# An RWKV and Hadamard feed-forward block: the third token form's down product is split once more, and the next tokens' chores move between engines

## The chip, the cores and the metric

The kernel runs on one core of a Trainium2 chip. A core has TensorE (matmuls into eight PSUM banks of 128 partitions x 512 fp32), VectorE, ScalarE, GpSimd, and SyncE, which here does nothing but issue DMAs. Each works through its own queue in order and waits on semaphores for the others. The metric is the device time of one execution in microseconds (us), as the median of several runs. The times spoken of inside an execution come from one profiled run.

In the profile the engines are PE (TensorE matmul), PEld (TensorE weight load), DVE (VectorE), ACT (ScalarE), POOL (GpSimd) and SP (SyncE). All instructions are recorded under line 34, since a small wrapper issues them, so the tile names tell them apart.

## The reference

Input x is 4 batches x 2048 tokens x 512 channels, fp32. Output is x plus an attention branch plus a feed-forward branch, both of the layer norm of x:

```python
xn = layernorm(x)                                   # over the 512 channels
shifted = xn, one token later (zero before the first)
xr, xk, xv = (mu * xn + (1 - mu) * shifted for mu in (mu_r, mu_k, mu_v))
r, k, v = xr @ Wr.T, xk @ Wk.T, xv @ Wv.T           # 512 x 512 each
wkv = recurrence over time of (k, v) with decay w and bonus u
attn = (sigmoid(r) * wkv) @ Wo.T
hidden = silu(xn @ W1.T) * (xn @ W3.T)              # 2048 wide
ffn = fwht(hidden) @ W2.T                           # Walsh-Hadamard, then back to 512
out = x + attn + ffn
```

## The kernel before

The 8192 tokens go through in eight blocks of 1024 (`TB`), with channels on partitions (`xnT`) and tokens along the free dimension. Matmuls are fp32; each matmul of the source is two in the trace. The Hadamard transform is folded into the second feed-forward weight in block 0, which also stores derived weights in HBM (`part_w`, `down_w`); block 1 derives and stores `deep_w`. From block 2 on all weights are only loaded.

Products of a 2 x 2 split (channels by tokens) are done with seven instead of eight block products, in the manner of Strassen and Winograd (`seven`, line 333): sums of the token quarters on the right, sums of weight quarters on the left, and the partial results passed between PSUM banks by ScalarE copies.

A block has two stages.

**Up stage.** In blocks 1 to 7 first six projected pairs (`projected_pair`, line 391; two each of k, v and r), then sixteen gate and linear tiles (`up`, line 421). Each of these 22 takes 28 matmuls of 512 columns. Between them, in small pieces handed out by `step` and `hook`, VectorE and ScalarE mix the tokens for v and r (`mix_before` on ScalarE, then `mix_here` on VectorE, then four differences in `mix_forms`) and run the recurrence (`wkv`, line 247, nine pieces for each of four channel groups). GpSimd makes the four token forms of the gate and linear tiles in `tf` (`token_forms`, line 310). Every tile loads the weights of the second next into a ring of three (`ring_a`). The results stand in `right`: sixteen units of gated hidden values and four of attention values (`r_of`), that is two halves of ten units, each by two token halves, named y11, y12, y21, y22.

**Down stage.** These 20 units are contracted to the 512 outputs, again with a seven-product split. In block 0 (`down_whole`, line 617) each of the seven is done whole, as four pieces of weights with five matmuls of 512 columns each. In blocks 1 to 7 (`down`, line 706) five of the seven (d0 to d4, class `Deep`, line 667) are split once more into seven products of 256 columns, each one piece of weights; the other two, T1 (form 0) and T3 (form 3), are done whole. `DEEP` (line 511) lists the weight forms that are split. The order of pieces is written out by hand in `program` (line 535), and the order of everything else in the body of `down`: `forms` are VectorE differences of 128 x 1280 elements, `step` is one product with its ScalarE copy, `clear` zeroes half a bank by ScalarE, `onto` adds a finished result (one PSUM addition of 512 columns and one of 256 from `s5`) to the output slots x11, x12, x22, x21, and `store` writes a slot out. Weights of the down stage come through a ring of eight pieces, `pieces_w`: at product u, piece u + 7 is asked for, once product u - 1 has left its slot.

The next block's tokens are prepared during the down stage by a generator, `next_tokens`, advanced at set places by `advance`. VectorE takes the statistics from `x_tok`, which lies in `k_sb` (`token_statistics`, line 144: bn_stats, bn_aggr, one power by GpSimd), two DMAs pass them through HBM and spread them over all partitions into `v_sb` (`statistics`, line 159), VectorE normalises `xnT` (eight pieces), mixes k's tokens into `tf` and makes three of their four forms.

All DMAs are issued by SyncE in the order of the program, so a DMA that has to wait holds those after it.

Of the kernel before, what the change touches and what calls it, by code (L numbers as in the profile page):

```python
# [1 line left out]

# [6 lines left out]
F32 = mybir.dt.float32  # L9
# [30 lines left out]
def tile_rwkv_attn_hadamard_ffn(  # L40
# [38 lines left out]
    deep_w = dram.tile([5, 7, P, QR, P], F32, name="deep_w")  # L79
# [39 lines left out]
    x_tok = k_sb.rearrange("p b t -> p (b t)").rearrange("p (t c) -> p t c", c=C)  # L119
# [4 lines left out]
    mix_of = {1: tf.rearrange("p f k t -> p (f k t)").rearrange("p (b t) -> p b t", t=TB)}  # L124
    mix_of[2], mix_of[0] = right[:, 0, 0:NB, :], right[:, 0, NB : 2 * NB, :]
    t4_of = {kind: unit(NP + n) for n, kind in enumerate((1, 2, 0))}
# [32 lines left out]
    def statistics(i):  # L159
        rs = token_statistics(i, x_tok)  # L160
        sp.dma_start(out=stat_d[i].rearrange("s (p t) -> p s t", p=P), in_=rs)
        sp.dma_start(out=spread, in_=stat_d[i].unsqueeze(0).to_broadcast([P, 2, TB]))

# [17 lines left out]
    def load_first_tokens(t, m):  # L181
        src = x[ds(t * P, m * P), :].rearrange("(t p) c -> p t c", p=P)
        sp.dma_start(out=x_tok[:, t : t + m, :], in_=src)

    def first_statistics(half):
        return token_statistics(f"f{half}", x_tok[:, half * HT : (half + 1) * HT, :])
# [123 lines left out]
    def token_forms():  # L310
        sub = ALU.subtract
        pool.tensor_tensor(t1, b12, b11, sub)
        pool.tensor_tensor(t2, b22, t1, sub)
        pool.tensor_tensor(t3, b22, b12, sub)
        pool.tensor_tensor(t4, b21, t2, sub)
# [195 lines left out]
    DEEP = (1, 4, 6, 5, 2)  # L511
# [24 lines left out]
    for m, n in ((1, 1), (2, 0), (1, 2), (2, 1), (1, 3), (1, 4), (2, 2), (1, 5), (2, 3), (2, 4), (2, 5), (1, 6), (2, 6)):  # L536
        program += deep(m, n)
    for m, n in ((3, 0), (3, 1), (4, 0), (3, 2), (4, 1), (3, 3), (3, 4), (4, 2), (3, 5), (4, 3), (4, 4), (3, 6), (4, 5)):
        program += deep(m, n)
    p7 = plain(3)  # L540
    program += [p7[0], *deep(4, 6), *p7[1:]]
# [75 lines left out]
    def down_whole(i, advance, next_parts):  # L617
# [8 lines left out]
        advance(1)  # L626
        next_parts()

# [7 lines left out]
        advance(8)  # L636
# [4 lines left out]
        advance(4)  # L641
# [9 lines left out]
        advance(3)  # L651
# [6 lines left out]
        advance(7)  # L658
# [8 lines left out]
    class Deep:  # L667
        def __init__(self, down, m, banks_of, rights, slots):
            self.m = m
            self.down, (self.a, self.b, self.f), self.q, self.t = down, banks_of, rights, slots  # L670
            self.s5 = small.tile([P, H // 2], F32, tag="s5", name=f"s5_{down.i}_d{m}")

        def clear(self):
            for pt in (self.a, self.f):
                act.activation(pt[:, lo], had_sb.unsqueeze(1).to_broadcast([P, 2, P]), AF.Copy, scale=0.0)
# [25 lines left out]
        def onto(self, slots, *which):  # L701
            for g in which:
                add(slots[g], (self.a, self.b)[g])
                dve.tensor_tensor(slots[g][:, hi], slots[g][:, hi], self.s5, ALU.add)

    def down(i, advance, next_parts, last):
# [4 lines left out]
        free = [s.rearrange("p f k c -> p (f k c)")[:, 0 : QR * (H // 2)].rearrange("p (q t) -> p q t", q=QR) for s in (  # L711
            ring_a.tile([P, 7, KH, P], F32, tag="a", name=f"right_{i}_{n}") for n in range(3))]
        k_flat, tf_flat = k_sb.rearrange("p b t -> p (b t)"), tf.rearrange("p f k t -> p (f k t)")
        in_k, in_tf = (
            [flat[:, ds(n * QR * H // 2, QR * H // 2)].rearrange("p (q t) -> p q t", q=QR) for n in range(3)]
            for flat in (k_flat, tf_flat)
        )
        d0 = Deep(d, 0, sets[0], y21, [*free, in_tf[0]])
        d1 = Deep(d, 1, sets[1], y11, [*in_k, in_tf[1]])
        d2 = Deep(d, 2, sets[0], y22, [*free, in_tf[2]])  # L720
        d3 = Deep(d, 3, sets[1], y22, [*in_k, y22[2]])
        d4 = Deep(d, 4, sets[0], y21, [*free, y21[2]])

        def forms(out, x0, x1, n):
            difference(out[n], x0[n], x1[n])

        def first(g, rh):
            d.plain_step(0, g, rh, pa, (0, 0), True)

# [7 lines left out]
        d1.clear()  # L737
        add(x11[0], pa[0])
        advance(1)
        d0.step(0, 1)  # L740
        first(1, 0)
        for n in (0, 1):
            forms(y11, y12, y11, n)
        d1.forms(0)
        d0.step(2)
        for n in (0, 1):
            forms(y12, y22, y12, n)
        first(1, 1)
        add(x11[1], pa[1])
        for g in range(KH):  # L750
            act.copy(u2_of[g], pa[g])
        for n in (2, 3):
            forms(y11, y12, y11, n)
        d1.forms(1)
        d0.step(3, 4)
        d0.onto(x11, 0)
        d1.forms(2, 3)
        d0.step(5)
        d1.step(0)
        d0.step(6)  # L760
        for n in (2, 3):
            forms(y12, y22, y12, n)
        d2.forms(0)
        d0.onto(x11, 1)
        d2.clear()
        d2.forms(1)
        d1.step(1)
        d2.step(0)
        d2.forms(2, 3)
        d1.step(2)  # L770
        d2.step(1)
        d1.step(3, 4)
        for n in (0, 1):
            forms(y22, y22, y11, n)
        for g in range(KH):
            d.store(x11[g], 0, g, 0)
        d1.onto(x12, 0)
        d1.onto(x22, 0)
        d2.step(2)
        d3.forms(0)  # L780
        d1.step(5)
        advance(2)
        d2.step(3)
        forms(y22, y22, y11, 3)
        d2.step(4)
        forms(y22, y22, y11, 2)
        d2.onto(x12, 0)
        d.residual(x21, 1, 0)
        d2.step(5)
        d3.clear()  # L790
        for n in (0, 1):
            forms(y21, y21, y22, n)
        d1.step(6)
        d1.onto(x12, 1)
        d1.onto(x22, 1)
        d2.step(6)
        d2.onto(x12, 1)
        d3.step(0)
        d4.clear()
        d3.step(1)  # L800
        d3.forms(1)
        d4.forms(0)
        d4.step(0)
        for n in (3, 2):
            forms(y21, y21, y22, n)
# [5 lines left out]
        advance(2)  # L811
        d3.step(4)
        d3.forms(3)
        d4.step(2)
        d4.forms(2)
        d3.onto(u2_of, 0)
        act.copy(pa[0], u2_of[0])
        d3.step(5)

        def c12(g):  # L820
            add(x12[g], u2_of[g])
            d.store(x12[g], 0, g, 1)

        c12(0)
        d4.step(3)
        advance(2)
        d4.step(4)
        d4.forms(3)
        d3.step(6)
        d3.onto(u2_of, 1)  # L830
        act.copy(pa[1], u2_of[1])
        c12(1)
        d4.step(5)
        d4.onto(x21, 0)
        d.plain_step(3, 0, 0, pa, (0, 1))
        advance(2)
        d4.step(6)
        d4.onto(x21, 1)
        next_parts()
        advance(7)  # L840

        def ends(pt, g, cols=whole):
            for slots, half in ((x22, 1), (x21, 0)):
                add(slots[g], pt, cols)
                d.store(slots[g], 1, g, half, cols)

        d.plain_step(3, 0, 1, pa, (0, 1))
        ends(pa[0], 0)
        if not last:
            for rh in range(2):  # L850
                d.plain_step(3, 1, rh, pa, (0, 1))
            ends(pa[1], 1)
            return
        other = sets[0][2]
        act.copy(other[:, hi], pa[1][:, hi])
        for pt, cols in ((pa[1], lo), (other, hi)):
            for rh in range(2):
                d.matmuls(pt, d.u + rh, quarter(0, 1, rh, cols), cols)
            ends(pt, 1, cols)
# [28 lines left out]
    pending = {}  # L888
    for i in range(n_blocks):
# [10 lines left out]


        tail = ()
        if i == 0:
            for kind, after in ((1, 2), (2, 0), (0, None)):
# [5 lines left out]
                if kind == 2:  # L910
                    token_forms()
# [15 lines left out]
            parts = [load_parts(i, 3 * KH + n) for n in range(2)]  # L927
        else:

# [10 lines left out]
            for kind in (1, 2) if i == 1 else (1,):  # L940
                next(pending[kind])
            chores, hooks = mix_chores(0) if i == 1 else mix_chores(2, 0), [0]
            for n in range(3 * KH):
                parts.append(load_parts(i, n + 2))
                if n == KH:
                    token_forms()

                def hook():
                    hooks[0] += 1
                    for _ in range(1 if i == 1 or hooks[0] % 3 else 2):  # L950
                        next(chores, None)
                    if hooks[0] in (9, 11, 12, 14, 15, 17, 18):
                        step()

                tail = projected_pair(i, n, parts.pop(0), tail, hook)


        for j in range(NF):
            if j + 2 < NF:
                parts.append(load_parts(i, 3 * KH + j + 2))  # L960
# [9 lines left out]
            if i == 1 and j in (3, 5, 7, 9, 11):  # L970
                keep_deep(j // 2 - 1, t)
            if i == 1 and j in (1, 3, 5, 7, 9):
                t = deep_forms(j // 2)
# [3 lines left out]
            tail = up(i, j, parts.pop(0), tail, step)  # L977
# [89 lines left out]
```

## Time and profile before

| | us |
|---|---|
| median of 3 runs (3058.1 to 3061.19) | 3058.76 |
| the profiled execution | 3057.26 |
| its span, first to last instruction | 3055.4 |
| TensorE busy | 3037.9 |
| VectorE busy | 2438.9 |
| ScalarE busy | 935.3 |
| GpSimd busy | 289.7 |

The granted TensorE clock is 0.999 of full speed. Waits are put down to what ended last. In a row of a group of instructions the columns are line, engine, operation, output and input tiles with shapes, count, then busy us, mean ns of one, and the engine's idle time just before them with what ended it.

Block 3 shows the stages: its up stage ends at 1444.1 us and its down stage at 1554.0.

### The profile page before, as it was taken

The page shows a single profiled execution, that of the slowest core. Times are in us where ns is not written, and L with a number is a line of the kernel's source. Part 1 is how long each engine was busy: PE and PEld are TensorE (multiplying, and loading weights), DVE is VectorE, ACT ScalarE, POOL GpSimd, SP SyncE. Part 2 cuts the span into 40 slices and gives each one's busy share as a digit, 9 for nine tenths or more (in the row PEclk, how much of TensorE's full clock was granted, in tenths as well). Part 3 has the DMA queues.
Part 4 walks back from the last instruction along what each step waited for, and adds up shares of the span by engine and source line. Part 5 has one row for each costly group of instructions (what it writes and reads, how often), then busy time and mean ns, then how long its engine had stood idle before and what let it go on. Part 6 is the DMA issues. An engine that isn't in the chain of part 4 may idle for free.

```text
span 3055.4 us, 23721 instructions
## 1 busy us (share of the span) xinstructions
PE 3037.9 (99%) x8302; PEld 1576.7 (52%) x8302; DVE 2438.9 (80%) x2594; ACT 935.3 (31%) x1571; POOL 289.7 (9%) x195
## 2 busy tenths in 40 slices
PE   8999999999999999999999999999999999999999
PEld 3444444447544475444844448444484445844457
DVE  6798847898688896788867888679786887868875
ACT  4233123331333313433133331433213332143320
POOL 3363103310100001000010000100001000010000
PEclk9999999999999999999999999999999999999999
DMA  4264523655322353223532245222462225522234
GB/s 174 74 204 169 183 99 123 215 215 173 119 80 77 131 184 115 73 79 132 191 102 83 73 142 186 102 74 83 152 192 86 73 74 183 159 86 85 72 119 134
DMA packets 131686, 387.11 MB, mean 127 GB/s; under 512 B 13936, under 2 KB 32624, under 8 KB 129392
## 3 DMA queue, kind: packets, MB, share of 16 engines
q1 hardware_dynamic: 131568, 385.60, 37.0%
q8 instruction: 67, 1.10, 0.1%
q14 instruction: 51, 0.42, 0.0%
HBM read 327.89 MB, written 57.66 MB: 126 GB/s over the span
## 4 chain that ended last, share of the span: by engine, by line
PE 98%; DVE 2%; DMA 0%; SPq 0%; ACT 0%; issue 0%; DVEq 0%; ACTq 0%
PE bank L34 98%; DVE right L34 0%; DVE e1b L34 0%; DMA xnT<-xT 0%; DVE xnT L34 0%; DVE e L34 0%; DVE sb L34 0%; DVE bank L34 0%; DVE tf L34 0%; SPq L34 0%; DVE sa L34 0%; DVE v_sb L34 0%; DVE k_sb L34 0%; ACT right L34 0%; ACT tf L34 0%
## 5 line engine op out<-in xcount | busy, mean ns | idle before, releaser
L34 PE MATMUL bank<-tf,part 128*128 128x512 f32 x2272 | 1042.2, 592 | 0.0
L34 PE MATMUL bank<-right,pieces_w 128*128 128x256 f32 (+1 forms) x2808 | 818.0, 451 | 0.0
L34 ACT COPY bank<-bank 128x512 f32<-128x512 f32 (+1 forms) x618 | 329.7, 534 | 1444.0 <-PE bank L34 1403.8
L34 PE MATMUL bank<-xnT,part 128*128 128x512 f32 x1536 | 722.1, 592 | 1.0 <-DVE right L34 1.0
L34 PEld LDWEIGHTS bank<-tf,part 128*128 128x128 f32 x2272 | 431.6, 190 | 543.4 <-issue 514.0
L34 PEld LDWEIGHTS bank<-right,pieces_w 128*128 128x128 f32 x2808 | 533.4, 190 | 275.3 <-issue 224.3
L34 PEld LDWEIGHTS bank<-xnT,part 128*128 128x128 f32 x1536 | 291.6, 190 | 369.3 <-issue 361.6
L34 DVE TENSOR_TENSOR right<-right 128x1280 f32<-128x1280 f32 (+2 forms) x215 | 308.3, 1465 | 21.7 <-PE bank L34 20.7
L34 DVE SCALAR_TENSOR_TENSOR right<-right,bank 128x512 f32<-128x512 f32 x256 | 174.0, 680 | 161.9 <-ACT right L34 161.6
L34 PE MATMUL bank<-right,part 128*128 128x512 f32 x616 | 272.3, 594 | 0.0
L34 ACT ACTIVATE right<-bank 128x512 f32<-128x512 f32 x308 | 183.9, 600 | 121.5 <-PE bank L34 102.1
L34 DVE RECIPROCAL e1b<-e1b 128x512 f32<-128x512 f32 x64 | 214.1, 3347 | 1.1
L34 DVE TENSOR_TENSOR bank<-bank,s 128x512 f32<-128x512 f32 x256 | 167.9, 690 | 35.7 <-ACT bank L34 25.2
L34 PEld LDWEIGHTS bank<-right,part 128*128 128x128 f32 x616 | 116.0, 190 | 149.4 <-issue 138.0
L34 DVE TENSOR_TENSOR right<-right,bank 128x512 f32<-128x512 f32 x256 | 173.6, 678 | 11.5 <-PE bank L34 7.1
L34 POOL TENSOR_TENSOR rs<-rs,neg_half 128x8 f32<-128x8 f32 x7 | 11.5, 1640 | 1372.7 <-DVE rs L34 1372.7
L34 DVE SCALAR_TENSOR_TENSOR right<-xnT,vec,right 128x1024 f32<-128x1024 f32 x64 | 85.1, 1358 | 67.1 <-ACT right L34 67.1
L34 ACT COPY s<-bank 128x512 f32<-128x512 f32 x128 | 74.9, 585 | 145.1 <-PE bank L34 145.1
L34 POOL TENSOR_TENSOR tf<-xnT 128x1024 f32<-128x1024 f32 x16 | 45.4, 2839 | 708.3 <-PE bank L34 708.3
L34 POOL TENSOR_TENSOR part<-part 128x256 f32<-128x256 f32 x88 | 93.9, 1078 | 173.4 <-DMA part<-wpart 90.3
L34 DVE TENSOR_TENSOR v_sb<-bank,v_sb 128x512 f32<-128x512 f32 (+1 forms) x91 | 61.7, 679 | 51.4 <-PE bank L34 51.4
L34 PE MATMUL bank<-pieces_w,part 128*128 128x512 f32 x224 | 100.7, 592 | 0.0
(109 smaller groups left out, 2331.5 us busy)
## 6 DMA issues: line engine op xcount, KB each, us to landing
part<-part_w SPq DMA_DIRECT2D x148, 896.0 KB, 4.6
pieces_w<-deep_w SPq DMA_DIRECT2D x245, 320.0 KB, 3.0
pieces_w<-down_w SPq DMA_DIRECT2D x104, 320.0 KB, 5.1
part_w<-part SPq DMA_DIRECT2D x22, 896.0 KB, 6.0
k_sb<-x SPq DMA_DIRECT2D x7, 2048.0 KB, 8.0
xnT<-xT SPq DMA_DIRECT2D x7, 2048.0 KB, 7.5
v_sb<-xT SPq DMA_DIRECT2D x48, 256.0 KB, 3.4
out<-v_sb SPq DMA_DIRECT2D x47, 256.0 KB, 2.2
```

The costliest lines, as they stand in the source:

```text
L34: return self.tc.keep_in_program_order(issue(*args, **kwargs))
```

## The change

T3 (weight form 3) becomes a sixth split product, d5: `DEEP`, `deep_w`, `deep_forms` and `keep_deep` get one entry more, and the last four pieces of `program`, whole ones, go. Its result is needed in both x22 and x21, so `onto` now takes several slots. Where d3's result (u2) was copied back into T3's banks, it is now added to x12, x22 and x21 by VectorE (`with_u2`).

The statistics of the next tokens are taken by ScalarE: for each of eight token groups one copy that accumulates the sum and one square, with the negative mean as bias, that accumulates the sum of squares; four small GpSimd operations make the factor and the offset of these. `x_tok` lies in `tf` instead of `k_sb`, except for the first tokens. The token forms for the gate and linear tiles are made by VectorE in the down stage.

Blocks 1 to 7 begin with gate and linear tile 0, and only then do the pairs follow. Only the ScalarE half of k's mixing is done in the down stage before; the VectorE half comes at the block's start and the four k forms in and after tile 0. After block 0 the mixed tokens lie in other units of `right`. Block 1 mixes v's tokens in the pairs like the later blocks.

```diff
-    DEEP = (1, 4, 6, 5, 2)
+    DEEP = (1, 4, 6, 5, 2, 3)
...
-    x_tok = k_sb.rearrange("p b t -> p (b t)").rearrange("p (t c) -> p t c", c=C)
+    x_first, x_tok = (flat.rearrange("p (t c) -> p t c", c=C) for flat in (k_flat, tf_flat))
...
+    mix_later = {1: right[:, 0, NB : 2 * NB, :], 2: right[:, 1, 0:NB, :], 0: right[:, 1, NB : 2 * NB, :]}
+    t4_of = {kind: unit(1 + n) for n, kind in enumerate((1, 2, 0))}
...
     def statistics(i):
-        rs = token_statistics(i, x_tok)
+        sums = small.tile([P, 2, TP], F32, tag="sums", name=f"sums_{i}")
+        rs = small.tile([P, 2, TP], F32, tag="rs", name=f"rs_{i}")
+        mean = small.tile([P, TP], F32, tag="mean", name=f"mean_{i}")
+        for t in range(TP):
+            tok = x_tok[:, t, :]
+            act.activation(tok, tok, AF.Copy, accum_out=sums[:, 0, t : t + 1])
+            yield
+        pool.tensor_scalar(mean, sums[:, 0, :], -1.0 / C, None, ALU.mult)
+        for t in range(TP):
+            tok = x_tok[:, t, :]
+            act.activation(tok, tok, AF.Square, bias=mean[:, t : t + 1], accum_out=sums[:, 1, t : t + 1])
+            if t + 1 < TP:
+                yield
+        pool.tensor_scalar(rs[:, 0, :], sums[:, 1, :], 1.0 / C, EPS, ALU.mult, ALU.add)
+        pool.tensor_tensor(rs[:, 0, :], rs[:, 0, :], neg_half, ALU.pow)
+        pool.tensor_tensor(rs[:, 1, :], mean, rs[:, 0, :], ALU.mult)
         sp.dma_start(out=stat_d[i].rearrange("s (p t) -> p s t", p=P), in_=rs)
         sp.dma_start(out=spread, in_=stat_d[i].unsqueeze(0).to_broadcast([P, 2, TB]))
+        yield
...
-    p7 = plain(3)
-    program += [p7[0], *deep(4, 6), *p7[1:]]
...
+        d1 = Deep(d, 1, sets[1], y11, [slot(v_flat), *in_k[0:2], in_tf[0]], s5[2])
+        d2 = Deep(d, 2, sets[0], y22, [*free, in_tf[1]], s5[1])
+        d5 = Deep(d, 5, (*pa, sets[1][2]), y12, [y12[0], in_tf[2], y12[1], y12[2]], s5[3])
...
+        d1.step(1)
+        chores.statistics(1)
+        d5.step(0)
+        d5.forms(0)
...
         d4.step(4)
         d4.forms(3)
+        d4.step(2)
+        d3.onto(0, u2_of)
+        with_u2(0)
+        d3.step(5)
+        chores.tokens(5)
+        d4.step(5)
+        next_parts()
+        chores.mix()
         d3.step(6)
+        d3.onto(1, u2_of)
+        with_u2(1)
+        d4.step(3)
+        d4.onto(0, x21)
+        d.store(x21[0], 1, 0, 0)
...
         d4.step(6)
+        left_over = lo if last else whole
+        d4.onto(1, x21, cols=(left_over,))
+        d.store(x21[1], 1, 1, 0, left_over)
...
-            for kind in (1, 2) if i == 1 else (1,):
-                next(pending[kind])
-            chores, hooks = mix_chores(0) if i == 1 else mix_chores(2, 0), [0]
+            for b in range(NB):
+                mix_here(1, b)
+            k_forms = mix_forms(1)
+            tail = up(i, 0, group(0), tail, lambda: next(k_forms))
+            for _ in k_forms:
+                pass
+            chores, hooks = mix_chores(2, 0), [0]
```

The new helpers in `down`, and the object that hands out the chores:

```python
        def with_u2(g):
            for slots, mh, half in ((x12, 0, 1), (x22, 1, 1), (x21, 1, 0)):
                add(slots[g], u2_of[g])
                if slots is not x21:
                    d.store(slots[g], mh, g, half)

    class Chores:
        def __init__(self, i):
            self.i = i
            self.of_statistics, self.of_tokens = statistics(i), chain(normalize(), token_forms(dve))
        def mix(self):
            mix_of.update(mix_later)
            for b in range(NB if self.i < n_blocks else 0):
                mix_before(1, b)
```

The order of the split products in the down stage from the twelfth piece on is, as (product, step): (1,1) (5,0) (1,2) (5,4) (2,0) (1,3) (1,4) (5,1) (2,1) (5,2) (1,5) (2,2) (5,3) (1,6) (2,3) (2,4) (5,5) (2,5) (5,6) (3,0) (2,6) (3,1) (4,0) (3,2) (4,1) (3,3) (3,4) (4,4) (4,2) (3,5) (4,5) (3,6) (4,3) (4,6).

## The prediction

> **What bounds the kernel.** I read the page's busy shares and the chain that ended last, then TensorE's own waits.
>
> ```profile
> PE 3037.9 (99%) x8302; PEld 1576.7 (52%) x8302; DVE 2438.9 (80%) x2594; ACT 935.3 (31%) x1571; POOL 289.7 (9%) x195
> ...
> PE 98%; DVE 2%; DMA 0%; SPq 0%; ACT 0%; issue 0%; DVEq 0%; ACTq 0%
> ```
> ```profile
> PE bank L34 <- DMA right<-w: 7.7, 1, 7.7
> PE bank L34 <- ACT right L34: 4.4, 1, 4.4
> PE bank L34 <- DVE right L34: 1.0, 2, 0.7
> PE bank L34 <- DVE tf L34: 0.9, 1, 0.9
> ```
>
> Total us, times, longest. The four waits add to 14.0 us; with 3.6 us after the last matmul they are all of the span that TensorE isn't busy (3055.4 - 3037.9 = 17.5). Only the 1.0 us "DVE right" lies behind the first 45 us, in block 1. So the time is a count of matmuls: a removed one is a gain at once, and any new wait is a loss at once.
>
> The timeline of TensorE in block 3's down stage (start, length) gives the price of a matmul.
>
> ```profile
> 1444.11 32.44 PE L34 MATMUL bank<-right,pieces_w 128*128 128x512 f32 x110
> ...
> 1478.54 2.32 PE L34 MATMUL bank<-k_sb,pieces_w 128*128 128x256 f32 x10
> 1480.70 2.32 PE L34 MATMUL bank<-right,pieces_w 128*128 128x256 f32 x10
> ...
> 1553.98 1.88 PE L34 MATMUL bank<-tf,part 128*128 128x512 f32 x4
> ```
>
> Ten matmuls of 256 columns are 2.16 us from start to start, 0.2158 each. The stage, 109.87 us, holds 80 of 512 and 350 of 256 columns (each matmul of the source is two in the trace): 109.87 - 350 x 0.2158 = 34.34, so 0.4293 for 512. The means of the group table (592, 379 ns) include the drain and are not used.
>
> **T3's product: the gain.** Removed per block 1 to 7: 4 pieces x 5 matmuls x 2 = 40 of 512 columns, 17.17 us. Added: 7 pieces x 5 x 2 = 70 of 256, 15.11 us. Gain 2.06 us, the stage becoming 107.8 us. In block 7 half of T3 was already cut by columns (20 and 40: 17.22 us), gain 2.11. Sum 6 x 2.06 + 2.11 = **14.5 us**.
>
> All else must hide behind TensorE. These rows price it (busy, mean ns).
>
> ```profile
> L34 DVE TENSOR_TENSOR right<-right 128x1280 f32<-128x1280 f32 x170 | 247.4, 1492 | 20.7 <-PE bank L34 20.7
> ...
> L34 DVE TENSOR_TENSOR v_sb<-bank,v_sb 128x512 f32<-128x512 f32 x89 | 60.9, 685 | 51.4 <-PE bank L34 51.4
> ...
> L34 DVE BATCH_NORM_STATS2 st<-k_sb 128x6 f32<-128x512 f32 x56 | 33.9, 678 | 0.0
> ...
> L34 ACT ACTIVATE right<-right 128x512 f32<-128x512 f32 x28 | 16.1, 630 | 0.0
> ...
> L34 POOL TENSOR_TENSOR rs<-rs,neg_half 128x8 f32<-128x8 f32 x7 | 11.5, 1640 | 1372.7 <-DVE rs L34 1372.7
> ...
> L34 ACT ACT_TABLE_LOAD x1 | 1.3, 1283 | 0.7 <-PEq L1058 0.7
> ```
> ```profile
> 1444.10:1461.30 17.20, 17.20 (x52) 9.50 (x51) 14.00 (x27) 1.82 (x6) 1.64 (x1) 1.00 0.37 142
> 1461.30:1502.30 41.00, 41.00 (x182) 34.22 (x181) 37.53 (x33) 4.94 (x13) 0.00 (x0) 1.00 0.67 216
> 1502.30:1540.00 37.70, 37.70 (x166) 31.33 (x165) 30.86 (x33) 9.74 (x19) 0.00 (x0) 1.00 0.54 163
> 1540.00:1554.00 14.00, 14.00 (x37) 6.67 (x37) 10.59 (x11) 0.00 (x0) 0.00 (x0) 1.00 0.21 83
> ```
>
> The last table is the down stage in four stretches: length, then busy PE, PEld, DVE, ACT, POOL, and the clock (1.00), DMA share, GB/s.
>
> **VectorE in down.** Before: 93.0 busy of 109.9. Off go the statistics (8 x 0.6 + 1.0 = 5.8), four mixes (4.9) and three k forms (3.7). On come d5's four forms (4 x 1.41 = 5.6, start to start), its two evictions onto x22 and x21 (4 x 1.14 = 4.6) and four token forms (4 x 1.22 = 4.9). About 93.7 of 107.8: it fits, so order decides. I count from the stage's start and lay VectorE's queue against the program's 2.16 us steps. Each form is ready well before its product: d1's t1 at 21.6 for 34.5, d5's t2 at 42.8 for 53.9, d4's t1 at 82.4 for 84.1, the narrowest. ScalarE clears d3's bank by 74.4 for 75.5.
>
> **Statistics on ScalarE.** 16 instructions of 0.63 us (row right<-right) are 10.1 us, spread between 13 and 37 us, where ScalarE otherwise has about 6 us. The Trainium skill ("ScalarE: Activation LUTs", Rules for kernel authors) speaks against it: plain arithmetic belongs on VectorE, and an ACTIVATE costs about 0.3 us + 0.83 ns an element, 0.73 us here, so 11.6 us in all; the row decides, and either fits. The accumulator's read-out is in no row: between 0 and another 0.63 us each. At twice the price, 20 us, ScalarE fills the stretch and copies behind it slip about 1 us. I take the row. Below nothing is excluded: TensorE has no stall there to give back.
>
> The same page (Table sets) names copy as in every set but not Square. The trace has one table load in all. If Square shared no set with tanh, two switches a block, 2.66 us each by the page, would be 37 us of ScalarE, hidden between copies due 4 us apart or more. By row or by rule TensorE loses nothing; I take no switch.
>
> **Queues.** The token load (2 MB, 8.0 us issue to landing) goes to tf, so SP waits until the last up tile's matmul ends; residuals follow it. Behind that wait stand six residual loads, the first wanted by VectorE at 8.6, and piece 7, wanted at 23.7; at the 8 us of the load both come in time. The tokens, landing near 8 us, are wanted by ScalarE at 13. The last Square follows at 37.7; four small GpSimd operations replace one, three of them behind it: 1.64 by the row and twice 1.0 by its 128x4 form (1013 ns), 41.5; the statistics' write and spread are issued by 43.8, spread landed near 49, wanted by VectorE at 54.7 (behind it there: d5's first eviction, which nothing needs soon). Behind that wait on SP stands piece 20: issued 43.9, landed 47 to 49, needed at 51.8. Margin 3 us; each us beyond is TensorE's, per block.
>
> **The start of a block.** With T = 0 at down's end: from T = -12.8 VectorE never rests: d4's last form 1.41, first half of u2's evictions 3.1, five token operations 6.1, second half 3.1, d4's two evictions 2.3, ending at T = 3.2; then four mixes of 1.22 to T = 8.1. ScalarE's four mix halves end at -1.7. The first up tile runs 12.02 us. Its third product needs a copy into the bank that d4's first eviction frees at T = 2.1; copied by 2.7, needed at 3.43: **0.7 us of margin**. The k forms f1, f2, f3 end at 10.1, 12.7, 14.0; the k products want them at 13.7, 15.5, 18.9. Its weights are issued at T = -8.3, behind u2's stores, and take 4.6 us. No stall, but nothing spare.
>
> **Once.** Block 1 makes a sixth deep form: four GpSimd operations (2.25 us each) more. Such a group costs VectorE 1 to 3 us, and VectorE there was late already (the 1.0 us wait). The next two tiles leave it 5 us: 0 to 3, I take 0.5. The end: u2's evictions now stand before the last store, and VectorE's last add ends 1.2 us behind the last matmul instead of 0.8: +0.4.
>
> **Sum.** Span 3055.4 - 14.5 + 0.5 + 0.4 = 3041.8; the profiled execution took 3057.26, 1.9 more, and the median of the three runs, 3058.76, is another 1.5 above that: **3045.2 us**.
>
> **Rivals.**
> (B) Small stalls eat part: the 0.7 us margin, or SP's piece, missed by about 0.7 us in most blocks. 7 x 0.7 = 5 us: 3050. For it: both margins are shorter than VectorE's error over 16 us of work. Against: VectorE resynchronises with TensorE at T = -12.8.
> (C) The gain is just eaten, by 2 us a block: 3059, no change. It needs VectorE 2.7 us late at T = 0.
> (D) Slower: VectorE's backlog at the start of a block. If it comes to T = 0 later than I laid out by x, TensorE loses x - 0.7 in each of six blocks; the gain is gone at x = 3.0 and it is slower by 0.2% from x = 4. At x = 6: 6 x 5.3 = 31.8 - 13.6, 3077. For it: 16 us without a gap, and nothing of the mixing was behind the last eviction before. Against: the rows' durations repeat within 0.1 us, and GpSimd, whose work stretches VectorE's, is quiet there.
> (E) The split itself doesn't pay. At 0.245 us a matmul the gain is nil, 3060; 2490 of this width at 0.2158 are against it.
>
> **Numbers.** A change of 0.2% (6 us) is about what can be told from none. Main case 0.68, its own range 3043.5 to 3047.5; B 0.10; C 0.07; D 0.14; E 0.01. Faster: A and B, 0.78; same (C and E) 0.08; slower 0.14. Leaving out D, E and the far half of C, the range is 3042.5 to 3055.
>
> **What the new profile would show.** Down stages of 107.8 us; 2940 matmuls of 256 columns (2490 before); TensorE waiting under 3 us behind the first 45 us; no group of batch-norm statistics but the first; one table load. A wait of TensorE on a ScalarE bank copy right at a block's start is B or D; on a transfer of pieces, SP's chain. Wrong would be any wait that comes back in each block for 2 us or more.

## The result, and the profile after

The change costs time. The kernel after takes **3063.8 us** (median of 20 runs, 3060.42 to 3068.71), the kernel before 3058.68 in the same comparison (3057.08 to 3062.41). The ratio is **1.0016, 95% interval 1.0009 to 1.0023**: slower by about 5 us, a difference inside the 0.2% that the prediction took as the least that can be told, yet clear of 1. The forecast was 3045.2, with 3042.5 to 3055 as its range. The profiled execution has a span of 3060.7 us against 3055.4, 5.3 more.

The page's busy shares and chain of the kernel after (its wrapper stands on line 35):

```profile
PE 3027.3 (99%) x8492; PEld 1615.3 (53%) x8492; DVE 2471.0 (81%) x2579; ACT 1014.1 (33%) x1822; POOL 233.0 (8%) x192
...
PE 86%; DVE 1%; DMA 1%; POOL 0%; ACT 0%; issue 0%; SPq 0%; DVEq 0%
```

TensorE is busy 10.6 us *less* than before (3037.9), though it runs 190 matmuls more: the saving is there. But the idle part of the span has grown from 17.5 to 33.4 us. The chain isn't followed to the start this time: it goes back from the end to 361.66 us and stops there, at SP's write of the statistics, so its 86% can't be set against the 98% of before. TensorE's own waits say what is new (total us, times, longest):

```profile
PE bank L35 <- DMA pieces_w<-down_w: 11.8, 1, 11.8
PE bank L35 <- DMA right<-w: 9.9, 1, 9.9
PE bank L35 <- ACT right L35: 3.9, 1, 3.9
PE bank L35 <- DVE v_sb L35: 2.5, 1, 2.5
```

Two of these rows have no counterpart before: 11.8 us once for down weights, and 2.5 us once for a VectorE instruction on `v_sb`. The timeline shows the first at 369.39 us, in block 0, and the second at 3055.25, before the last product. Neither recurs from block to block.

What makes up the 5.3 us, from the two timelines:

| | us |
|---|---|
| T3's product by the matmul count (512 columns: 5812 before, 5552 after; 256 columns: 2490 and 2940; at 0.4293 and 0.2158) | -14.5 |
| block 0's wait for down weights, 369.39 (11.8 idle by the row, 12.0 from start to start) | +12.0 |
| six matmuls after it at half rate (0.80 to 1.01 us instead of 0.43) | +2.6 |
| last product: waits 2.6, but the span's end follows the start of the last matmul by 3.4 instead of 4.0 | +2.1 |
| start: k's first product after the fold at 45.72 instead of 44.43 | +1.3 |
| two waits of 0.31 for a deep piece (1136.13, 1508.89) | +0.6 |
| remainder, in many small gaps, not followed | +1.2 |

The start is no part of the change: between the profiled executions of this case in which it holds the same work, that moment lay anywhere from 44.2 to 48.3 us. So one wait, once, in the block that the change was not aimed at, with its aftermath, eats the whole gain.

Here is how it comes about, in block 0's down stage of the kernel after. The timeline's columns are start, length, engine, line, operation, output and input, count, and in brackets the idle time before and what ended it. First what SyncE issues:

```profile
337.06 0.38 SPq L35 DMA_DIRECT2D xnT<-xT  x1
337.49 0.50 SPq L35 DMA_DIRECT2D part<-part_w  x1
338.04 0.42 SPq L35 DMA_DIRECT2D part<-wpart  x1
...
361.68 0.37 SPq L35 DMA_DIRECT2D stat_d<-rs  x1
...
363.65 0.86 SPq L35 DMA_DIRECT2D pieces_w<-down_w  x2
```

Then GpSimd, ScalarE and TensorE over the same time:

```profile
348.03 5.33 POOL L35 TENSOR_TENSOR part<-part 128x256 f32<-128x256 f32 x4 [66.44 <-DMA part<-wpart]
353.33 0.24 POOL L35 TENSOR_SCALAR mean<-sums 128x8 f32<-128x8 f32 x1
353.60 0.72 ACT L35 ACTIVATE tf<-tf,mean 128x512 f32<-128x512 f32 x1 [20.54 <-POOL mean L35]
...
359.71 1.67 POOL L35 TENSOR_TENSOR rs<-rs,neg_half 128x8 f32<-128x8 f32 x1
361.45 0.20 POOL L35 TENSOR_TENSOR rs<-mean,rs 128x8 f32<-128x8 f32 x1
...
369.39 7.10 PE L35 MATMUL bank<-right,pieces_w 128*128 128x512 f32 x10 [11.81 <-DMA pieces_w<-down_w]
```

Read it from the top. SP asks for block 1's weight parts only at 337.49, because ahead of them in its queue stands the load of `xnT`, which waits for VectorE's copy of the last token column. The parts land at 348. GpSimd adds them up until 353.36, and only then comes to the mean, whose eight sums ScalarE had had ready since about 333: its first Square waited 20.54 us for that mean. Eight squares, two GpSimd operations, and at 361.68 SP can write the statistics. It had stood at that write since 338.5, and behind it stands the next pair of down pieces. They are issued at 363.65 and land at 369.35; TensorE had wanted the first at 357.4.

In the kernel before, SP's queue in the same place reads:

```profile
343.26 0.37 SPq L34 DMA_DIRECT2D stat_d<-rs  x1
345.21 0.90 SPq L34 DMA_DIRECT2D part<-wpart  x2
346.21 1.12 SPq L34 DMA_DIRECT2D pieces_w<-down_w  x2
```

Statistics first, parts second, and pieces at 346.21, 17.4 us earlier. The diff exchanged these two steps in block 0: `advance(1)` did the statistics before `next_parts()`; now `chores.start()` and `next_parts()` come before `chores.statistics(2 * TP)`.

### The profile page after: what moved, and what is told of

Read it like the earlier page. It is cut to its first block, busy times and chain, and to the rows that moved or that the text cites. A ratio compares the mean times of both kernels' runs of the same rounds, so it can differ in the third digit from the quotient of the medians.

```text
span 3060.7 us, 24403 instructions
## 1 busy us (share of the span) xinstructions
PE 3027.3 (99%) x8492; PEld 1615.3 (53%) x8492; DVE 2471.0 (81%) x2579; ACT 1014.1 (33%) x1822; POOL 233.0 (8%) x192
## 4 chain that ended last, share of the span: by engine, by line
PE 86%; DVE 1%; DMA 1%; POOL 0%; ACT 0%; issue 0%; SPq 0%; DVEq 0%
PE bank L35 86%; DMA pieces_w<-deep_w 0%; DVE e1b L35 0%; POOL rs L35 0%; DVE right L35 0%; DMA pieces_w<-down_w 0%; DMA stat_d<-rs 0%; DVE sa L35 0%; DVE v_sb L35 0%; DVE e L35 0%; DVE bank L35 0%; DVE sb L35 0%; ACT tf L35 0%; SPq L35 0%; ACT s_d L35 0%
## 5 line engine op out<-in xcount | busy, mean ns | idle before, releaser
L35 PE MATMUL bank<-tf,part 128*128 128x512 f32 x2048 | 941.9, 592 | 0.0
L35 PE MATMUL bank<-right,pieces_w 128*128 128x256 f32 (+1 forms) x2928 | 792.5, 431 | 14.6 <-DMA pieces_w<-down_w 11.8
L35 PEld LDWEIGHTS bank<-right,pieces_w 128*128 128x128 f32 x2928 | 557.5, 191 | 242.9 <-issue 167.9
L35 PEld LDWEIGHTS bank<-tf,part 128*128 128x128 f32 x2048 | 389.6, 190 | 489.6 <-issue 461.8
L35 DVE TENSOR_TENSOR right<-right 128x1280 f32<-128x1280 f32 (+2 forms) x236 | 328.9, 1420 | 64.7 <-PE bank L35 63.7
L35 PE MATMUL bank<-right,part 128*128 128x512 f32 x840 | 369.6, 594 | 0.0
L35 PEld LDWEIGHTS bank<-right,part 128*128 128x128 f32 x840 | 158.6, 190 | 203.0 <-issue 189.2
L35 DVE SCALAR_TENSOR_TENSOR right<-xnT,vec,right 128x1024 f32<-128x1024 f32 x92 | 119.7, 1337 | 14.3 <-ACT right L35 14.3
L35 ACT ACTIVATE right<-xnT,omm 128x1024 f32<-128x1024 f32 x92 | 100.3, 1143 | 12.3 <-PE bank L35 12.3
L35 PE MATMUL bank<-k_sb,pieces_w 128*128 128x256 f32 x420 | 97.5, 379 | 0.0
```

The lines of the kernel that those rows point to most:

```text
L35: return self.tc.keep_in_program_order(issue(*args, **kwargs))
```

## The experiments

The theory: the exchanged order and GpSimd's extra part in the statistics (it now stands before *and* behind ScalarE's squares) together make block 0's wait, and the rest of the prediction holds. Rivals: the ScalarE statistics alone are too late whatever the order; the loss lies in the deep stages, where the gain was to be; or the gain of T3's split isn't 14.5. Medians are of several runs, a single figure is one run; the before beside them lay at 3058.3 to 3058.6 each time.

**1. Parts after the statistics, in block 0 only.**

```diff
-        next_parts()
         chores.statistics(2 * TP)
+        next_parts()
```

> One line of block 0's down stage is moved: the first two weight loads of block 1 (with the four GpSimd sums of the second) are asked for after the statistics of the next tokens, not before. Theory (order on GpSimd): the negative mean stands behind those sums, which wait for their weights, and everything behind it waits in turn. With the order turned, the mean runs near 333 us instead of 353, the statistics' write is issued near 341 instead of 362, and TensorE's 11.8 us wait at 369 goes, with the 2.6 us of half-speed matmuls after it: 14.5 us off, some 3049 us against 3058.7 before. Rival (the statistics on ScalarE are themselves too slow, or the 4 MB of token transfers hold the weights up): the wait stays, at 5 us or more, time above 3056.

Measured: 3049.94 us (3047.26 to 3052.01), ratio 0.9971 (0.9959 to 0.9982). SP in block 0:

```profile
344.97 0.37 SPq L35 DMA_DIRECT2D stat_d<-rs  x1
...
348.80 1.06 SPq L35 DMA_DIRECT2D pieces_w<-down_w  x2
```

The mean is made at 335.77, 17.6 us earlier, the pieces are asked for 14.9 us earlier, and TensorE doesn't wait for them. By the medians two lines in another order are worth 13.9 us, against 14.6 counted in the trace of after (12.0 + 2.6). With the order mended the change as a whole is a gain.

**2. Order as changed, but block 0's statistics by VectorE as before.**

```diff
...
+        if i == 1:
+            rs = token_statistics(i, x_tok)
+            sp.dma_start(out=stat_d[i].rearrange("s (p t) -> p s t", p=P), in_=rs)
+            sp.dma_start(out=spread, in_=stat_d[i].unsqueeze(0).to_broadcast([P, 2, TB]))
+            for _ in range(2 * TP):
+                yield
```

> In block 0 alone the statistics of the next tokens are taken by VectorE again, as in the kernel before; the order of the queues stays that of the changed kernel. Theory (order on GpSimd): the one power on GpSimd still stands behind the four sums until 353 us; write, spread and the weights follow at 355, 357 and 358 and land near 363, so TensorE still waits some 5 to 6 us there; time 3055 to 3058. Rival (ScalarE's statistics are the cause): the wait is gone, 3049.

Measured: 3053.47 us, span 3051.4. GpSimd, and TensorE's wait:

```profile
346.93 3.01 POOL L35 TENSOR_TENSOR part<-part 128x256 f32<-128x256 f32 x4 [66.52 <-DMA part<-wpart]
```
```profile
PE bank L35 <- DMA pieces_w<-down_w: 3.4, 1, 3.4
```

The wait stays, smaller: from start to start 3.56 us and 1.75 more in slow matmuls, 5.3 in all against 14.6. So the order alone costs about 5 us even with VectorE's statistics, whose one GpSimd operation (at 349.89) also stands behind the sums of the parts; that ScalarE's chain needs GpSimd twice, with eight squares between, makes up the other 9.

**3. Order as changed, but the last Square and what follows it later.** The statistics' tail, with SP's write, then comes behind product 1 and two residual loads.

```diff
-        chores.statistics(2 * TP)
+        chores.statistics(2 * TP - 1)
...
         d.residual(x22, 1, 1)
+        chores.statistics(1)
```

> The order of the changed kernel stays, but in block 0 the last of the sixteen statistics pieces (last square, three GpSimd operations, the write and the spread) comes one product later, so that four more weight pieces stand in front of the write in SyncE's queue. Theory (GpSimd's delay reaches TensorE through SyncE's queue alone): the mean still runs only at 353 us, yet the wait at 369 goes and with it 14.5 us: 3049. Rival (the delay reaches TensorE by ScalarE's or VectorE's queue, or by the transfers): a wait of several us stays.

Measured: 3049.09 us, span 3047.3. SP:

```profile
337.07 0.99 SPq L35 DMA_DIRECT2D pieces_w<-down_w  x2
...
360.47 0.38 SPq L35 DMA_DIRECT2D stat_d<-rs  x1
```

The mean is as late as in after (352.11 for 353.33) and so are the statistics (360.47 for 361.68), and TensorE has no wait in block 0. What hurt was only that the piece stood behind the write in SP's queue; late statistics by themselves cost TensorE nothing here.

**4. The parts ahead of everything.** `next_parts()` before `chores.start()`, hence before the load of `xnT`.

```diff
+        next_parts()
         chores.start()
-        next_parts()
         chores.statistics(2 * TP)
```

> The changed kernel, with the weight loads of block 1 asked for ahead of the channel load as well, so ahead of SyncE's wait for VectorE's copy. Refined theory: the four sums are done by 345 us, the statistics go through by 350, and the 11.8 us wait with its 2.6 us is gone: about 3049 us, as in the first run. Rival (the sums ahead of the mean are enough to delay it, whenever their weights come): a wait of several us stays.

Measured: 3047.74 us (3046.5 to 3052.96), ratio 0.9967 (0.9954 to 0.998).

```profile
322.75 0.42 SPq L35 DMA_DIRECT2D part<-wpart  x1
337.81 0.38 SPq L35 DMA_DIRECT2D xnT<-xT  x1
...
347.55 0.86 SPq L35 DMA_DIRECT2D pieces_w<-down_w  x2
```

The parts come first here too, as in after, but they are asked for 15.3 us earlier; GpSimd has done its sums by 334.95, the mean follows at once, and there is no wait. So "parts before statistics" isn't what costs: it is parts *between* the `xnT` load, which waits for VectorE, and the statistics.

**5. The kernel before, parts first.** `next_parts()` ahead of `advance(1)`:

```diff
-        advance(1)
         next_parts()
+        advance(1)
```

> The kernel before with the two lines of block 0's down stage turned the other way: the two weight loads of block 1 with their eight GpSimd sums are asked for ahead of the next tokens' statistics. Nothing else of the change is in it. Theory (the order on GpSimd alone makes the loss): the power runs near 359 us instead of 341, SyncE holds the down stage's weights until 362, and TensorE waits some 10 us near 357, with 2.6 us at half speed after it: about 3071 us. Rival (the order hurts only together with ScalarE's statistics or the later token load): no wait, 3058.

Measured: 3058.74 us, span 3057.0, no wait in block 0. The expected loss didn't come.

```profile
324.23 4.49 SPq L34 DMA_DIRECT2D part<-wpart  x2
339.10 0.38 SPq L34 DMA_DIRECT2D xnT<-xT  x1
```

My edit had moved the parts ahead of the `xnT` load as well, since one `advance(1)` does both load and statistics. It is the case of experiment 4 in the old kernel, and agrees with it.

**6. The kernel before, in exactly the order of after.** The generator hands back control once more after the load of `xnT` in block 0:

```diff
         advance(1)
         next_parts()
+        advance(1)
...
             load_channels(i + 1)
+            if i == 0:
+                yield
             statistics(i + 1)
```

> The kernel before, with block 0's down stage in exactly the changed kernel's order: the channel load of the next tokens, then the two weight loads of block 1 with their eight GpSimd sums, then the statistics (VectorE's, as before). In the fifth run the weights had gone ahead of the channel load too, which waits for a copy by VectorE; there the sums began at 334 us and were done before the power was wanted. Refined theory (the weights stand behind the channel load in SyncE's queue, so the sums are late, so the power is late, so SyncE holds the down stage's weights): weights asked for at 336, sums from 346 to 358, the write near 361, and TensorE waits about 11 us near 357 with 2.6 us at half speed after it: about 3071 us. Rival (the order can't hurt a kernel with VectorE's statistics): no wait, 3059.

Measured: 3064.18 us (3062.86 to 3067.97, 15 runs), ratio 1.002 (1.0012 to 1.0028); before 3058.53. SP, GpSimd, and TensorE's wait:

```profile
335.98 0.97 SPq L34 DMA_DIRECT2D part<-wpart  x2
352.18 0.38 SPq L34 DMA_DIRECT2D stat_d<-rs  x1
354.16 0.86 SPq L34 DMA_DIRECT2D pieces_w<-down_w  x2
```
```profile
344.37 5.98 POOL L34 TENSOR_TENSOR part<-part 128x256 f32<-128x256 f32 x8 [64.17 <-DMA part<-wpart]
```
```profile
PE bank L34 <- DMA pieces_w<-down_w: 4.1, 1, 4.1
```

With nothing else of the change the order costs the old kernel 5.65 us by the medians; the trace shows a wait of 4.3 from start to start and 1.6 of slow matmuls, 5.9. The size was expected at about twice this: I had let GpSimd finish the sums near 358, and they were done at 350.35. Experiments 1, 2, 4, 5 and 6, with before and after, fill this table of what waiting for block 0's pieces cost TensorE, in us by the traces:

| | statistics, then parts | parts ahead of the `xnT` load | parts behind the `xnT` load, then statistics |
|---|---|---|---|
| statistics by VectorE | 0 (before) | 0 (experiment 5) | 5.9 (experiment 6), 5.3 (experiment 2) |
| statistics by ScalarE and GpSimd | 0 (experiment 1) | 0 (experiment 4) | 14.6 (after) |

In block 0 neither part of the change costs anything without the exchanged order; with it, ScalarE's chain more than doubles the price. "ScalarE's statistics alone" falls as a rival.

**7. T3 whole again, on top of experiment 1.** This asks whether T3's split is worth what its count says.

```diff
-    DEEP = (1, 4, 6, 5, 2, 3)
+    DEEP = (1, 4, 6, 5, 2)
...
-        d5.step(0)
-        d5.forms(0)
+        d.plain_step(3, 0, 0, pa, (0, 1), True)
...
-        d5.onto(0, x22, x21)
+        add(x22[0], pa[0])
+        add(x21[0], pa[0])
```

> As the first of these runs, but T3's product is done whole again, at the places of the split one (four pieces with 512 columns for seven with 256; its sums and its deep form are left out). Theory: the split is worth 17.17 - 15.11 us in each of seven blocks and nothing else hangs on it, so this run is 14.4 us slower than the first one, about 3063 us. Rival (narrow products pay less, or bring waits of their own that the first run hides in its sum): the difference is under 10 us.

Measured: 3068.92 us (3067.45 to 3070.31), ratio 1.0032 (1.0019 to 1.0045). It is 19.0 us above experiment 1 where 14.4 was expected. The surplus is a wait that my placing of T3's four pieces made:

```profile
PE bank L35 <- ACT bank L35: 5.3, 7, 0.8
```

Seven times, once a block, TensorE waits for a ScalarE copy; with the gaps' full lengths, 0.92 each, that is 6.4 us. The two profiled spans are 3067.1 and 3050.2, 16.9 apart: 14.5 by the count (280 of 512 columns for 490 of 256) and 6.4 for these waits, less 2.4 by which this start was earlier and 2.1 that experiment 1's execution lost more in block 1, to deep pieces and at the end, make 16.4; the other 0.5 lies in small gaps. So the count fits, but since this kernel isn't free of stalls of its own, the run supports the gain rather than measures it. The cleaner evidence is experiment 9 below.

**8. The last product without its early half, on top of experiment 1.** The second half of the last output tile is added and stored together with the first, after the last product.

```diff
-        if last:
-            d4.onto(1, x21, cols=(hi,))
-            d.store(x21[1], 1, 1, 0, hi)
         d4.step(6)
-        left_over = lo if last else whole
-        d4.onto(1, x21, cols=(left_over,))
-        d.store(x21[1], 1, 1, 0, left_over)
+        for cols in (hi, lo) if last else (whole,):
+            d4.onto(1, x21, cols=(cols,))
+            d.store(x21[1], 1, 1, 0, cols)
```

> As the first run of this study (weights of block 1 asked for after the statistics), and in the last block the upper half of the last output slot is no longer added and stored ahead of the last product. Theory: the last product waits 2.6 us because VectorE still reads the other half of the same bank, and the wait makes its ten matmuls slow (some 1.5 us); without the early half both go, the last stores come 0.9 us later after it: 3 us off, about 3047 us. Rival (the wait is for the weights or for ScalarE's copy): it stays, and the time rises by the 0.9 us.

Measured: 3046.39 us (3045.21 to 3047.4), ratio 0.9958 (0.9945 to 0.997), 3.5 below experiment 1 by the medians. The wait of 2.5 us on `v_sb` has gone from TensorE's waits.

**9. Also the last Square earlier in the deep stages.** The last Square and the GpSimd operations go one product earlier; SP's two DMAs stay where they were.

```diff
         pool.tensor_tensor(rs[:, 1, :], mean, rs[:, 0, :], ALU.mult)
+        yield
         sp.dma_start(out=stat_d[i].rearrange("s (p t) -> p s t", p=P), in_=rs)
...
-        chores.statistics(2 * TP)
+        chores.statistics(2 * TP + 1)
...
+        chores.statistics(1)
         d1.step(1)
```

> As the run before, and the last square of the statistics with its GpSimd operations stands ahead of the copy of product (1,1) on ScalarE, only the two DMAs stay behind it. Theory: the write of the statistics is issued about 3 us earlier in each of blocks 1 to 6, piece 20 lands in time, and its waits of 0.2 to 0.4 us in some blocks go: 0 to 2 us off, about 3046 us. Rival (the piece is late for the load on the DMA rings, not for its issue): the small waits stay.

Measured: **3044.71 us** (3042.91 to 3047.35), ratio **0.9955 (0.9942 to 0.9969)**, span 3042.7. Its waits of TensorE:

```profile
PE bank L35 <- DMA right<-w: 7.7, 1, 7.7
PE bank L35 <- ACT right L35: 3.9, 1, 3.9
...
PE bank L35 <- DVE right L35: 1.1, 2, 0.9
PE bank L35 <- DVE tf L35: 0.9, 1, 0.9
```

These are the waits of the kernel before, row for row; no wait for a deep piece is left. Against experiment 8 the step itself is small (1.7 us by the medians, whose ranges overlap). This version beats both kernels, and its span is within 0.9 us of the 3041.8 that the prediction's sum gave. Against before, T3's count takes 14.5 off, its start came 1.25 us later (45.68 for 44.43), its end takes 0.46 more and block 1's wait 0.13 more: 3055.4 less 12.7 is 3042.7, the measured span.

## Why the prediction was wrong

**The failed step is "Queues".** It walked the chain token load, sums, squares, GpSimd, statistics' write, piece behind it on SP, but only in the split down stage of blocks 1 to 7. There the mean has a free GpSimd, and piece 20 was to have 3 us of margin. Block 0 has a down stage of its own, `down_whole`, with the same steps in another order, and that stage wasn't walked at all. In it the chain passes twice through a GpSimd queue that holds block 1's weight sums, these wait for a load that waits for another load that waits for VectorE, and the step "behind that wait on SP stands piece" came true for piece 11 instead of piece 20: 12.0 us and 2.6 of slow matmuls (after; experiments 1, 3, 4 and 6 show the order, the queue and the place). Rival B named the mechanism, a piece held on SP, at 0.7 us in most blocks; it was 14.6 once. Of the signs that the prediction named, the wait on a transfer of pieces is the one that came; a wait that comes back in each block for 2 us or more, which it named as wrong, did not.

**Mis-sized in the same step: GpSimd and the piece's transfer in the deep stages.** The three operations behind the last Square were put at 3.6 us. Block 2 in after, then two links of its chain (start, length):

```profile
1122.09 0.85 POOL L35 TENSOR_SCALAR rs<-sums 128x8 f32<-128x8 f32 x1 [14.64 <-ACT tf L35]
1123.02 2.91 POOL L35 TENSOR_TENSOR rs<-rs,neg_half 128x8 f32<-128x8 f32 x1
1126.01 1.46 POOL L35 TENSOR_TENSOR rs<-mean,rs 128x8 f32<-128x8 f32 x1
```
```profile
1129.55 6.54 DMA pieces_w<-deep_w
1136.13 357.51 PE bank L35 x1006
```

From the first start to the last end that is 5.4 us, where the same three in block 0 take 2.2 (359.43 to 361.65): 0.20, 1.67 and 0.20 there, 0.85, 2.91 and 1.46 here. VectorE runs its 128x1280 differences of two SBUF inputs, 1.49 us each, at that time. The Trainium skill ("SBUF — State Buffer", Summary: rules for kernel authors) says that of such an instruction and a GpSimd instruction that reads SBUF the second to issue blocks until the first has finished; increments of 0.65, 1.24 and 1.26 us, each below one such difference, agree. I had priced the power at 1.64 from rows where it ran undisturbed. So piece 20 was asked for 45.4 us after the stage's first matmul (1084.13) instead of 43.9. The rest of the margin went in the transfer: it landed 6.54 us after its issue, where 3 to 5 were laid out. The margin of 3 us became about nothing, and two blocks lost 0.31 each.

**Mis-sized: the end.** "Once" gave +0.4; it was +2.1. The early addition of half of the last tile stands behind u2's three additions on VectorE, which is busy without a pause from 3051.45 on, and the last product waits for it:

```profile
3054.78 0.42 DVE L35 TENSOR_TENSOR v_sb<-bank,v_sb 128x256 f32<-128x256 f32 x1
...
3055.25 2.43 PE L35 MATMUL bank<-right,pieces_w 128*128 128x256 f32 x10 [2.48 <-DVE v_sb L35]
```

The addition reads columns 256 to 511 of a bank, the product writes columns 0 to 255 of the same bank. The wait is one of the program: in the trace the product's first weight load waits for a semaphore that this addition raises at its end. I had counted VectorE's work behind the last matmul but not this wait ahead of it. Experiment 8 takes the wait out.

**Right: the gain of T3.** 2940 matmuls of 256 columns, as said. Block 2's down stage in after, first matmul and the first of the next stage:

```profile
1084.13 8.32 PE L35 MATMUL bank<-right,pieces_w 128*128 128x512 f32 x19
...
1192.36 1.88 PE L35 MATMUL bank<-xnT,part 128*128 128x512 f32 x4
```

108.23 us, with one of the 0.31 waits in it: 107.9, predicted 107.8. The span of experiment 9 says the same of all seven blocks.

**Right: the start of a block.** At block 3's start, where T = 0 is 1192.36, VectorE ends its evictions and mixes as follows:

```profile
1194.65 0.42 DVE L35 TENSOR_TENSOR v_sb<-v_sb,s_d 128x256 f32<-128x256 f32 x1
1194.99 4.87 DVE L35 SCALAR_TENSOR_TENSOR right<-xnT,vec,right 128x1024 f32<-128x1024 f32 x4
```

The last eviction ends at T = 2.7 (3.2 laid out), the mixes at 7.5 (8.1), ScalarE's halves at -1.75 (-1.7). TensorE's waits have no row for a bank copy by ScalarE, so the 0.7 us of margin held in every block and rivals C and D, which hung on a late VectorE, didn't happen. **The sixth deep form** in block 1 was put at +0.5: its wait is 1.4 us against 1.3 before.

**Right: ScalarE's statistics and the table.** By form, the squares, the copies' read-outs and the table load (busy, mean ns, idle before and its releaser):

```profile
L35 ACT ACTIVATE tf<-tf,mean 128x512 f32<-128x512 f32 x56 | 40.1, 717 | 26.0 <-POOL mean L35 26.0
...
L35 ACT ACTIVATION_READ_ACCUMULATOR tf<-tf 128x1 f32 x56 | 10.7, 190 | 0.0
...
L35 ACT ACT_TABLE_LOAD x1 | 1.3, 1283 | 0.7 <-PEq L1117 0.7
```

Square made no table switch. The read-out, bounded between 0 and 0.63 us, is an instruction of its own of 0.19 us, and the squares, 0.72 long, follow one another at 0.70 to 0.71 us. ScalarE's mix halves, which have no read-out, are 1.14 long and follow one another at 1.05, so a read-out costs less than 0.1 of pitch. Of the prediction's two prices, its estimate of 0.73 fits the squares (717 ns) and the row's 0.63 the copies (621 ns). These steps hid as laid out in blocks 1 to 6, which alone take statistics there. The 26.0 us of idle ScalarE ahead of the squares are the mark of block 0: 20.5 of them are the one wait for the mean there.

## What to carry to other kernels

A step that is shared by several stages has to be walked through each stage's queues as they stand in that stage, the one-off first stage too: here the exchange of two lines in the stage that runs once cost 14.6 us and the main idea in the seven others saved 14.5. Where one engine issues all DMAs in order, ask of each DMA that waits for computation what stands behind it, and keep weights for the bottleneck ahead of results that nobody needs soon. A chain that visits a lightly used engine twice pays that engine's queue twice.

## What the runs showed of the hardware that I had not expected

**After a wait TensorE ran at half rate for a while.** Two stretches of after, block 0's wait and the time behind it, then the second of these in experiment 1, and last the end of experiment 1 (length, busy PE, PEld, DVE, ACT, POOL, granted clock, DMA share, GB/s):

```profile
357.00:369.30 12.30, 0.58 (x2) 0.00 (x0) 0.00 (x0) 2.82 (x9) 2.06 (x3) 0.66 0.35 135
369.30:375.40 6.10, 6.01 (x8) 2.57 (x9) 0.30 (x1) 0.00 (x0) 0.00 (x0) 0.57 1.05 408
```
```profile
369.30:375.40 6.10, 6.10 (x15) 2.66 (x14) 3.65 (x4) 0.00 (x0) 0.00 (x0) 1.00 0.37 106
3043.35:3046.76 3.41, 3.41 (x9) 2.70 (x9) 0.15 (x1) 0.00 (x0) 0.00 (x0) 0.50 0.32 115
```

In the 6.1 us behind the wait the granted clock is 0.57, and 8 matmuls run where experiment 1 runs 15. They start at 369.39, 370.40, 371.25 and so on, 0.85 apart instead of 0.43. It cost 2.6 us after a wait of 12.0 (from start to start), 1.75 after one of 3.6 (experiment 2) and 1.6 after one of 4.3 (experiment 6), so some two thirds as much after the short ones. The Trainium skill ("TensorE: Matmul & The Clock Gate", What's actually happening) has the array throttled to half its clock after an idle window of about 3.4 us and released after as long a busy one; matmuls of 0.85 us in the place of 0.43 are what it describes. But less idle time can be enough: before the last product TensorE was idle for 2.48 us in six executions, and in four of them (experiments 1, 2, 3 and 7) its matmuls then ran at 0.43 instead of 0.22, with a granted clock of 0.50 in experiment 1 (the last row above), which cost 0.8 to 1.8 us in all; in the two others (after, experiment 4) they did not. What decides between them isn't shown. In these runs a wait of some 4 us cost TensorE about 1.4 to 1.5 times its length.

**GpSimd's small operations** took 0.6 to 1.3 us more each beside VectorE's two-input work, as shown above; a price from a row that ran alone is a lower bound. It goes the other way too: in the kernel before, VectorE's 128x1024 differences `right<-right` took 1.22 us with GpSimd idle and 2.08 on average (at most 2.77) where GpSimd's work lay over them.

**A VectorE read of one half of a PSUM bank held a product into the other half** (2.5 us at the end), through the program's semaphore, as the trace shows. Whether the chip would run the two side by side without that wait, no run here shows.
